# Scans of a four-direction state-space layer: the place of one exponential in ScalarE's queue

## The chip, the cores and the metric

The kernel runs on one core of one Trainium2 chip. The metric is the device time of one execution in microseconds (us). A change under about 0.2% can't be told from no change in this kernel.

## The reference

Two layers work on x, (4, 64, 64, 128) in float32: an attention, a recurrent layer, a selective scan in four directions, and a layer of experts. The change lies in the selective scan, whose core is, for each image b, direction k and channel d (256 channels, 16 states each, 4096 positions):

```
dt = softplus(dts + dt_proj_b)
def step(h, (dt_l, u_l, B_l, C_l)):
    dA = exp(dt_l[..., None] * A)
    h  = h * dA + (dt_l * u_l)[..., None] * B_l
    y  = einsum('bkdn,bkn->bkd', h, C_l)
```

The kernel computes the softplus of a value s as the larger of two numbers: ln(1 + e^s), and a lower bound 1 / (e^-s + 0.5).

## The kernel before, in words

The work of the scans stage (function `scans`) is cut into 132 **windows**: four directions, 33 windows each, of 4 blocks of 125 positions from the four images laid end to end. Of each window 16 **tiles** are scanned: four groups of states (4 of the 16 each), and in a group one tile for each of the four blocks. A tile holds 128 channels on the partitions, times 2 halves of the channels, 4 states and 127 columns, 1016 elements in a row.

One loop over p (the **turn**) writes out the order of all engines by hand, under `manual_schedule`: each engine executes its instructions in the order in which the loop issues them. Group g has the tiles at turns 4g + (g mod 2) + 0, 2, 4, 6, so two groups are interleaved and a tile's successor in its own group comes two turns later. Turns are counted within 16 here, since all repeats from window to window. At turn p the loop issues in this order:

- `finish` (at one turn of a window): a copy of the finished sums on ScalarE (L1415).
- `fill` of tile p+1: TensorE multiplies out the inputs of the scan into one of two PSUM buffers db (L1319), which the scan of tile p-1 must have left.
- `carry` of tile p-1: a small copy on ScalarE (L1364) of the last column of that tile's states into the decays of the tile that continues it. For the first three tiles of a group this is the tile two turns on (p+1 at the time of issue), for the last tile it is the first tile of the same states in the next window, ten turns after the tile. Tile 11 is the last of its group (5, 7, 9, 11); tile 12 is the third of its group (8, 10, 12, 14) and is continued by tile 14.
- `scan` of tile p on VectorE (L1343), which needs its db, its decays and the column carried in.
- sums on TensorE (L1394), the products with C on GpSimd (L1377), and a load of a later row of C on SyncE's queue.
- `decay`: up to three exponentials of decays on ScalarE (L1284), for a group that is scanned later.
- the steps of `project`, a generator which prepares a later window. Each `yield -n` in it says at which turn, counted from the window's own first one, the next step is issued; a step takes its place behind all else of its turn.

The steps of `project` around the change, all on ScalarE, work on tiles of 128 x 1000 elements. `pts` is a PSUM view that holds s; `e` and `bound` are SBUF tiles (`bound` is a view of the tile that the profile calls low; `pts` is a view of mm):

- turn -22 (10 within the window being scanned): `bound` = e^-s (L1200) and e = e^s (L1203), each with a maximum-check sum (`accum_out`).
- turn -21 (11): `bound` = ln(bound + 0.5) (L1205), `pts` = ln(1 + e) (L1206).
- turn -20 (12): `bound` = exp(-bound) (L1208), the last step of the lower bound.
- turns -19 and -18 (13 and 14): dt = max(`pts`, `bound`), in two halves on VectorE (L1214), each behind that turn's scan.
- turn -17: dt times u on GpSimd (L1217), turn -14 and -13: the diagonals of B on VectorE (L1232) and ScalarE (L1248).

`decay` issues three exponentials at turn 12, ahead of the step of turn -20, three at turn 13 and two at turn 14, all for the group whose first tile is scanned at turn 16. `flag` isn't None in the version that runs here; the other branch is for inputs out of range.

Of the kernel before, what the change touches and what calls it, by code (L numbers as in the profile page):

```python
# [20 lines left out]
AF = mybir.ActivationFunctionType  # L21
# [977 lines left out]
def scans(ctx, tc, a, us, ys, flag):  # L999
# [10 lines left out]
    nc = tc.nc  # L1010
# [126 lines left out]
    def in_halves(of):  # L1137
        return of.rearrange("p h (j t) -> p h j t", j=2)

    def project(v):  # L1140
# [46 lines left out]
        bound = in_halves(low[:, : ND * W].rearrange("p (h t) -> p h t", h=ND))  # L1187
        e = in_halves(e)
        if flag is None:
            nc.scalar.activation(e, pts, AF.Relu, scale=-1.0, bias=most)  # L1190
            nc.scalar.activation(e, e, AF.Exp, scale=-1.0, bias=most)
            nc.scalar.activation(bound, e, AF.Copy, scale=-0.5, bias=1.0)
            yield -21
            nc.gpsimd.tensor_mul(bound, bound, e)
            for h in range(ND):
                nc.vector.tensor_max(bound[:, h], pts[:, h], bound[:, h])
            nc.scalar.activation(pts, e, AF.Ln, bias=1.0)
        else:
            nth = todo.index(v)
            nc.scalar.activation(  # L1200
                bound, pts, AF.Exp, scale=-1.0, accum_out=largest[:, 1, nth : nth + 1]
            )
            nc.scalar.activation(e, pts, AF.Exp, accum_out=largest[:, 0, nth : nth + 1])  # L1203
            yield -21
            nc.scalar.activation(bound, bound, AF.Ln, bias=half)  # L1205
            nc.scalar.activation(pts, e, AF.Ln, bias=1.0)  # L1206
            yield -20
            nc.scalar.activation(bound, bound, AF.Exp, scale=-1.0)  # L1208
        yield -19
        v.dt = work.tile([P, ND, W], F32, tag="dt", name="dt")  # L1210
        dt = in_halves(v.dt)
# [16 lines left out]
        for turn, i in ((-14, 0), (-13, 2)):  # L1228
# [18 lines left out]
            for t in range(FEW + 4 * h, FEW + 4 * h + 4):  # L1247
# [4 lines left out]
                    scale=ident32[:, t : t + 1],  # L1252
# [181 lines left out]
    with tc.manual_schedule():  # L1434
# [3 lines left out]
        def projections(p):  # L1438
            nth, turn = divmod(p + BEFORE, TILES)
            if turn == 0 and nth < len(todo):  # L1440
                v = todo[nth]
                v.steps, v.starts = project(v), nth * TILES
                v.goes_on = next(v.steps)
                running.append(v)
            for v in list(running):
                while v.goes_on is not None and p - v.starts >= v.goes_on:
                    v.goes_on = next(v.steps, None)
                if v.goes_on is None:
                    running.remove(v)
# [455 lines left out]
```

## Time and profile before

| what | us |
|---|---|
| runs: median of 3 (lowest, highest) | 9323.02 (9310.93, 9323.11) |
| the profiled execution's own time | 9321.16 |
| its span, from the first to the last instruction | 9319.2 |
| first scan to last scan of the stage (2112 scans) | from 3598.6 to 8650.2 of the span |
| VectorE busy from 3595 to 8655 | 4960.65 of 5060 |
| GpSimd, TensorE, ScalarE busy there | 4842.52, 4798.82, 4536.72 |

The profile is of one execution. PE is TensorE, DVE is VectorE, ACT is ScalarE, POOL is GpSimd. A row of a timeline gives start, length, engine, line, operation, output and input, and the number of instructions that were merged into it. In brackets stands how long the engine stood idle before it, and whose work it waited for. An instruction's length runs on for about 0.07 to 0.1 us after its engine has taken the next one, so lengths add up to a little more than the time they take. In a merged row the length reaches from the first start to the last end.

### The profile page before, as it was taken

The numbers are of one execution on the slowest core, as the hardware profiler recorded it, in microseconds if no ns is written. First come the engines' busy times: TensorE is split into PE (matmuls) and PEld (weight loads), VectorE is DVE, ScalarE is ACT, GpSimd is POOL, SyncE is SP. The second block draws the span as 40 slices with busy tenths as digits, with TensorE's granted clock in tenths as the row PEclk, the third lists the DMA queues.
The fourth block names the chain that finished last, engine by engine and source line by source line (L and its number), as shares of the span: only waits on it lengthen the run. The fifth ranks groups of instructions, "written<-read, shape, count | busy, mean of one in ns | idle before, by whom it ended". The sixth has DMA issues, their size and how long they took to land. (4 is left out here: it accounts for less than half of the span.)

```text
span 9319.2 us, 241459 instructions
## 1 busy us (share of the span) xinstructions
PE 8594.7 (92%) x103250; PEld 4327.6 (46%) x103250; DVE 8279.5 (89%) x5102; ACT 7300.2 (78%) x12114; POOL 4960.2 (53%) x2433
## 2 busy tenths in 40 slices
PE   7999999999989886999999999999999999999766
PEld 3333333333323334555555555555555555555223
DVE  6999999999978415999999999999999999999754
ACT  3888888888856457999999998889999999898321
POOL 0000000000001015999999999999999999999100
PEclk8999999999989887999999999999999999999877
DMA  4000001000011234666666655566666666666624
GB/s 168 39 8 35 8 8 37 8 8 8 8 53 50 107 124 141 178 177 179 180 180 165 165 163 162 164 172 177 179 180 180 179 179 176 175 178 171 238 105 186
DMA packets 533040, 1164.78 MB, mean 125 GB/s; under 512 B 78930, under 2 KB 446546, under 8 KB 504164
## 3 DMA queue, kind: packets, MB, share of 16 engines
q1 hardware_dynamic: 531940, 1149.09, 41.7%
q8 instruction: 815, 13.35, 0.6%
q14 instruction: 285, 2.33, 0.1%
HBM read 828.29 MB, written 182.15 MB: 108 GB/s over the span
## 5 line engine op out<-in xcount | busy, mean ns | idle before, releaser
L1343 DVE TENSOR_TENSOR_SCAN states<-decays,db 128x1016 f32<-128x1016 f32 x2112 | 4657.3, 2255 | 45.8 <-PE db L1319 17.6
L1377 POOL TENSOR_TENSOR products<-states,c_ring 128x1000 f32<-128x1000 f32 x2112 | 4454.1, 2160 | 215.7 <-DVE states L1343 183.8
L1284 ACT ACTIVATE decays<-dt,a_logs 128x500 f32<-128x500 f32 x4224 | 3021.2, 715 | 87.3 <-DVE states L1343 1.2
L1319 PEld LDWEIGHTS db<-b_diag,dtu_t 32*128 32x128 f32 x16896 | 2048.0, 187 | 1388.7 <-DVE states L1343 1208.8
L1319 PE MATMUL db<-b_diag,dtu_t 32*128 32x128 f32 x16896 | 2438.3, 283 | 259.5 <-DVE states L1343 239.9
L1319 PE MATMUL db<-b_other,dtu_t 32*128 32x128 f32 x16896 | 2438.0, 283 | 0.0
L1328 PE MATMUL y<-zeros 32*128 32x128 f32 x14720 | 2123.2, 283 | 0.0
L1319 PEld LDWEIGHTS db<-b_other,dtu_t 32*128 32x128 f32 x16896 | 2047.6, 187 | 1.6
L1394 PE MATMUL y<-products,ident 64*64 64x500 f32 x16896 | 2022.3, 592 | 0.3 <-POOL products L1377 0.3
L1328 PEld LDWEIGHTS y<-zeros 32*128 32x128 f32 x14720 | 1773.4, 186 | 0.0
L342 DVE TENSOR_TENSOR total<-total,ring 128x2048 f32<-128x2048 f32 x768 | 1706.6, 2283 | 32.4 <-ACT ring L304 31.7
masks.py:197 POOL MEMSET ident<- 128x128 f32 x6 | 1.2, 205 | 2915.7 <-SPq L181 2623.3
L304 ACT ACTIVATE ring<-sa 128x2048 f32<-128x2048 f32 (+3 forms) x667 | 1153.7, 1738 | 274.6 <-PE sa L289 263.0
L314 PE MATMUL av<-ring,v_at 128*32 128x256 f32 (+1 forms) x16128 | 1096.3, 389 | 6.2 <-ACT o L323 5.7
L1394 PEld LDWEIGHTS y<-products,ident 64*64 64x64 f32 x16896 | 541.8, 132 | 697.4 <-issue 569.8
L314 PEld LDWEIGHTS av<-ring,v_at 128*32 128x32 f32 x16128 | 421.5, 109 | 951.6 <-issue 749.6
L304 ACT ACTIVATE ring<-sb 128x1536 f32<-128x1536 f32 (+2 forms) x585 | 800.7, 1375 | 73.0 <-PE sb L289 62.8
L289 PE MATMUL sa<-q_at,k_at 32*128 32x512 f32 x4898 | 701.7, 641 | 20.9 <-issue 14.8
L289 PE MATMUL sb<-q_at,k_at 32*128 32x512 f32 x3294 | 623.3, 640 | 0.0
L1248 ACT ACTIVATE b_diag<-mm,ident 128x64 f32<-128x64 f32 x1056 | 261.5, 375 | 322.9 <-DVE b_diag L1232 308.2
L1364 ACT COPY decays<-states 128x8 f32<-128x8 f32 x2048 | 405.2, 198 | 99.9 <-DVE states L1343 98.3
L289 PEld LDWEIGHTS sa<-q_at,k_at 32*128 32x128 f32 x4898 | 192.3, 183 | 354.8 <-issue 177.4
(218 smaller groups left out, 8069.9 us busy)
## 6 DMA issues: line engine op xcount, KB each, us to landing
c_ring<-c_rows SPq DMA_DIRECT2D x2112, 250.0 KB, 5.0
b_other<-b_diag SPq DMA_DIRECT2D x264, 512.0 KB, 5.2
weights<-in_w SPq DMA_DIRECT2D x32, 1024.0 KB, 13.0
u<-u_r SPq DMA_DIRECT2D x60, 500.0 KB, 6.5
y_r<-sum SPq DMA_DIRECT2D x60, 500.0 KB, 5.6
u<-u_c SPq DMA_DIRECT2D x60, 500.0 KB, 6.4
y_c<-sum SPq DMA_DIRECT2D x60, 500.0 KB, 5.3
x<-x SPq DMA_DIRECT2D x96, 256.0 KB, 2.6
```

Source lines behind the costliest of these rows:

```text
L289: nc.tensor.matmul(s[:, m, :], k[rows, tokens(t)], q[rows, chunk(chunk_state["c"])], start=True, stop=True,)
L304: nc.scalar.activation(ring[:, lo : lo + n, :], s[:, at : at + n, :], AF.Exp)
L314: nc.tensor.matmul(chunk_state["av"][rows, some], chunk_state["v"][:, t, rows], ring[:, at + i, some], start=t == 0, stop=t == NJ - 1 and ...
L342: nc.vector.tensor_add(sums[g % 2], sums[g % 2], w)
L1248: nc.scalar.activation(v.b_diag[:, :, :, t].rearrange("p s n -> p (s n)"), b_ps.rearrange("p s n -> p (s n)"), AF.Identity, scale=ident32[ ...
L1284: nc.scalar.activation(to, dt, AF.Exp, scale=scale)
L1319: nc.tensor.matmul(bank.rearrange("p (n t) -> p n t", n=4)[:, :, to : to + 32], v.dtu[rows, h, s, :], b[rows, s, 4 * self.q : 4 * self.q + ...
L1328: nc.tensor.matmul(y[:, idle // 2, :P], zeros[rows], zeros[rows], start=False, stop=False)
L1343: nc.vector.tensor_tensor_scan(order(self.slot(states)), order(self.slot(decays, shift)), order(self.db[:, SKIP + shift :][:, : 2 * LANE]) ...
L1364: nc.scalar.copy(self.edge(later.slot(decays), later.v.into), last)
L1377: nc.gpsimd.tensor_mul(to, h, c)
L1394: nc.tensor.matmul(to, ident[rows, rows], of, start=begins, stop=ends)
```

## The change

The step `bound` = exp(-bound) is issued at turn -21 instead of -20, between the two logarithms. The turn -20 has no step any more. No instruction is added or taken away, and nothing else moves.

```
@@ -1203,9 +1203,8 @@
             nc.scalar.activation(e, pts, AF.Exp, accum_out=largest[:, 0, nth : nth + 1])
             yield -21
             nc.scalar.activation(bound, bound, AF.Ln, bias=half)
+            nc.scalar.activation(bound, bound, AF.Exp, scale=-1.0)
             nc.scalar.activation(pts, e, AF.Ln, bias=1.0)
-            yield -20
-            nc.scalar.activation(bound, bound, AF.Exp, scale=-1.0)
         yield -19
```

ScalarE's order from turn 11 to turn 13 was: carry of tile 10, ln for the bound, ln(1+e), carry of tile 11, three decays, exp for the bound, carry of tile 12. It becomes: carry of tile 10, ln for the bound, exp for the bound, ln(1+e), carry of tile 11, three decays, carry of tile 12.

More of the change, by code (lines that the diff above doesn't have):

```diff
@@ L1205, in project @@
             nc.scalar.activation(bound, bound, AF.Ln, bias=half)
+            nc.scalar.activation(bound, bound, AF.Exp, scale=-1.0)
             nc.scalar.activation(pts, e, AF.Ln, bias=1.0)
-            yield -20
-            nc.scalar.activation(bound, bound, AF.Exp, scale=-1.0)
         yield -19
```

## The prediction

> **What bounds the kernel now.** I read the page first, for the stage that holds the change. Its slices give one digit per engine (tenths busy in 40 equal slices):
>
> ```profile
> PE   7999999999989886999999999999999999999766
> DVE  6999999999978415999999999999999999999754
> ACT  3888888888856457999999998889999999898321
> POOL 0000000000001015999999999999999999999100
> ```
>
> From slice 16 on, where the scans run, all four engines show 8 or 9, so none is free and the question is which one holds up the others in each turn. VectorE's waits from 3595 to 8655 us (the stage) answer it for the engine with the most work:
>
> ```profile
> DVE dt L1214 <- ACT low L1208: 62.7, 124, 14.0
> DVE states L1343 <- PE db L1319: 17.6, 12, 3.0
> DVE states L1343 <- ACT decays L1284: 3.1, 3, 2.3
> ```
>
> Columns: total us, times, longest. VectorE's one regular wait is that of the maximum (L1214) for the exponential which the change moves (L1208): 124 times, of which two come before the first scan (windows 0 and 1, the 14.0 among them), so 122 in the steady run. Then I read a window of 38.2 us, VectorE first:
>
> ```profile
> 6018.62 0.53 DVE L1232 TENSOR_TENSOR b_diag<-mm,ident 128x384 f32<-128x384 f32 x1
> 6019.15 22.15 DVE L1343 TENSOR_TENSOR_SCAN states<-decays,db 128x1016 f32<-128x1016 f32 x10
> 6041.66 0.68 DVE L1214 TENSOR_TENSOR dt<-mm,low 128x500 f32<-128x500 f32 x1 [0.35 <-ACT low L1208]
> 6042.25 2.26 DVE L1343 TENSOR_TENSOR_SCAN states<-decays,db 128x1016 f32<-128x1016 f32 x1
> 6044.43 0.65 DVE L1214 TENSOR_TENSOR dt<-mm,low 128x500 f32<-128x500 f32 x1
> ```
>
> The ten scans are tiles 4 to 13, the one at 6042.25 is tile 14. And ScalarE over the same turns:
>
> ```profile
> 6036.34 0.20 ACT L1364 COPY decays<-states 128x8 f32<-128x8 f32 x1
> 6036.43 1.13 ACT L1205 ACTIVATE low<-low,half 128x1000 f32<-128x1000 f32 x1
> 6037.46 1.00 ACT L1206 ACTIVATE mm<-e 128x1000 f32<-128x1000 f32 x1
> 6038.39 0.20 ACT L1364 COPY decays<-states 128x8 f32<-128x8 f32 x1
> 6038.48 2.22 ACT L1284 ACTIVATE decays<-dt,a_logs 128x500 f32<-128x500 f32 x3
> 6040.60 1.02 ACT L1208 ACTIVATE low<-low 128x1000 f32<-128x1000 f32 x1
> 6041.53 0.19 ACT L1364 COPY decays<-states 128x8 f32<-128x8 f32 x1
> ...
> 6047.29 0.20 ACT L1364 COPY decays<-states 128x8 f32<-128x8 f32 x1 [0.51 <-DVE states L1343]
> ```
>
> ScalarE runs without a pause from the second diagonal of B (L1232 ends at 6019.15) to 6047.29: over these turns it, and not VectorE, sets the pace. The exponential ends at 6040.60 + 1.02 = 6041.62, and the maximum starts 0.04 later.
>
> **The change, step by step.** *What the wait costs now.* The last of the ten scans ends at 6019.15 + 22.15 = 6041.30 and, being 2.25 long (the scan group's mean is 2255 ns), started at 6039.05. VectorE takes an unheld instruction 2.18 after a scan's start (6042.25 to 6044.43). So the maximum could start at 6041.23 and starts at 6041.66: 0.43 lost, a little more than the 0.35 of idle shown, since the scan's tail overlaps.
>
> *What becomes of it.* The maximum will need only the two logarithms and the exponential, all ahead of the carry of tile 11. The three together take 6036.43 to 6038.39 plus one exponential (6040.60 to 6041.53 is 0.93): done by about 6039.5, some 1.7 us before VectorE asks. This wait goes wholly.
>
> *What is late next.* The scan of tile 14 follows the maximum by 0.59 (6041.66 to 6042.25) and could start at 6041.82. But it needs the carry of tile 12, the copy that starts at 6041.53, and ends at 6041.72. Scans that are released by such a copy start 0.08 to 0.09 after its end: the copy before the scan at 6019.15 starts at 6018.86, takes 0.21 and so ends at 6019.07. With the same instructions in front of it, this copy would release the scan at 6041.81, just in time.
>
> *What the order itself costs.* The moved exponential reads and overwrites what the logarithm in front of it has just written. Before, ln(1+e) and four more instructions stood between. An instruction that isn't held starts about 0.10 before the former ends (L1205 ends at 6037.56, L1206 starts at 6037.46). One that waits for its predecessor doesn't: the three decays take 2.22, against 3 x 0.715 = 2.145, so 0.04 of gap at each of two steps. The difference, 0.10 + 0.04 = 0.14, is what I take for the new dependence; from below it is 0 (no wait is needed), from above some 0.2 (a dependence over a longer write, half as much again). No other pair changes its kind. So the carry of tile 12 ends at 6041.86 and releases the scan of tile 14 at 6041.94 to 6041.95. Against 6042.25 that is 0.31 gained a window, with 0.43 at the 0 end (VectorE itself then decides) and 0.24 at the 0.2 end.
>
> A rule bears on this step: the Trainium skill, "ScalarE: Activation LUTs", section "What ACT_TABLE_LOAD costs", says that back-to-back activations overlap by about 93 ns. The rows of unheld pairs agree (0.10), those of the decays, which are back to back too, don't (a gap of 0.04). By the rule alone the sum would be the 0 end.
>
> *Who else is delayed.* ln(1+e), the carry of tile 11 and the three decays come 0.93 + 0.14 = 1.07 later. ln(1+e) then ends at about 6039.5, as said. The carry of tile 11 feeds tile 21, since 11 is the last of its group, ten turns off. The three decays end at about 6041.8 and are for tile 16, scanned after 6047. None of them is on the path; if the carry of tile 11 were, see the slower rival. From the carry of tile 12 on, ScalarE is 0.14 later than now: its next carry (6043.73, for the scan at 6045.00) has over 0.7 to spare now and still has 0.5, since that scan moves to 6044.69. No DMA is moved, nor anything on SyncE's, GpSimd's or TensorE's queue.
>
> *Does the gain last?* ScalarE stands idle 0.51 at 6047.29 for a scan's end; 0.31 + 0.14 = 0.45 fits into that, so it then shifts with VectorE. Later in the window it waits 2.3 us for the diagonals, which VectorE sets. GpSimd waits for scans after its long row:
>
> ```profile
> 6044.59 2.15 POOL L1377 TENSOR_TENSOR products<-states,c_ring 128x1000 f32<-128x1000 f32 x1 [0.81 <-DVE states L1343]
> 6047.34 2.16 POOL L1377 TENSOR_TENSOR products<-states,c_ring 128x1000 f32<-128x1000 f32 x1 [0.59 <-DVE states L1343]
> ```
>
> That is 1.40 a window, of which 0.31 is used up. TensorE stands still for scans' ends after tiles 13, 14, 15 and 3 (L1319 waits for the states), so its chain starts anew from VectorE behind the change and shifts too. So the whole window becomes 0.31 shorter, about 37.8 instead of 38.15.
>
> *Sum.* 122 x 0.31 = 38 us. Against the profiled execution's 9321.2 this gives 9283; the runs' median is 1.9 higher, so 9285 in its terms. The ends: 122 x 0.43 = 52 (9271) and 122 x 0.24 = 29 (9294).
>
> **The rivals.** *The exponential isn't held by the logarithm* (the rule above): 9271, with a chance of 0.12. Only the decays' spacing speaks against it, and that is of other tiles.
>
> *The gain is absorbed*: the window is set elsewhere, by the PSUM fills (12 waits of scans for them, 17.6 us), or the order on ScalarE comes out as before. Then 9323. Against it: the waits of ScalarE, GpSimd and TensorE for VectorE, each longer than 0.31 a window in total. Chance 0.08.
>
> *The carry of tile 11 is wanted at once* (slower). If the scan of tile 13 needed it, as most scans need the copy one turn before, it would end at 6038.59 + 1.07 = 6039.66 and release the scan at 6039.74 instead of 6039.05, 0.69 late. With the maximum's wait gone (0.43) the window is 0.26 longer: 122 x 0.26 = 32 us, 9355. It decides as soon as the scan of tile 13, or anything before the maximum, is held by more than 0.43. For it: ScalarE has no pause in these turns, so all behind the moved step is 1 us late. Against it: the numbering of the tiles, and that the trace shows that scan unheld today. Chance 0.06, other things that make it slower included.
>
> **How the numbers follow.** The forecast has 0.74: 9285. About 0.2% (18.6 us) is what a measurement here can tell from no change, so faster means below 9304.4. Forecast and first rival lie there: 0.86. Same: 0.08. Slower: 0.06. The range reaches from below the first rival, as the runs differ among themselves by 12 us, to the edge of "same": 9264 to 9304. The absorbed and the slower case stay outside, with 0.14.
>
> **What the profile after should show.** The wait of L1214 for L1208 is gone from VectorE's list. The exponential starts about 0.04 after the end of the logarithm before it, ln(1+e) follows. The scan of tile 14 starts about 0.6 to 0.7 after the maximum, and 0.08 after the end of a carry; windows are 37.8 apart. Wrong: a new wait of the scan of tile 13 or 12 for ScalarE (the slower rival), a longer wait of L1319 or of scans for db (absorbed), the exponential 0.1 before the logarithm's end with windows of 37.7 (first rival).

## The result, and the profile after

The kernel with the change takes 9279.8 us (median of 5 runs, 9276.8 to 9283.0) against 9316.2 us before (median of 5, 9310.9 to 9323.1). The ratio is 0.9960, with a 95% interval from 0.9949 to 0.9971: faster, by 27 to 48 us, or 0.3 to 0.5%. The profiled execution took 9277.8 us, its span is 9275.8 against 9319.2, and the stage of the scans, from the first scan to the last, went from 5051.6 to 5010.3 us: 41 of the 43 us lie there.

In the new file the lines behind the change have moved up by one: the scan is L1342, the maximum L1213, the carry L1363, the decays L1283, the moved exponential is L1206 and ln(1+e) L1207. These are VectorE's longest waits in the stage (total us, times, longest):

```profile
DVE states L1342 <- issue: 11.2, 61, 0.4
DVE states L1342 <- PE db L1318: 10.2, 8, 2.2
DVE states L1342 <- ACT decays L1283: 7.7, 5, 4.6
```

The line on top of the list before, the maximum for the exponential, is gone. The new first line is not harmless: "issue" is where the list could name nobody, and the timeline shows who it is. VectorE in the same turns of one window:

```profile
5957.85 0.53 DVE L1231 TENSOR_TENSOR b_diag<-mm,ident 128x384 f32<-128x384 f32 x1
5958.39 22.15 DVE L1342 TENSOR_TENSOR_SCAN states<-decays,db 128x1016 f32<-128x1016 f32 x10
5980.45 0.65 DVE L1213 TENSOR_TENSOR dt<-mm,low 128x500 f32<-128x500 f32 x1
5981.19 2.27 DVE L1342 TENSOR_TENSOR_SCAN states<-decays,db 128x1016 f32<-128x1016 f32 x1
5983.37 0.65 DVE L1213 TENSOR_TENSOR dt<-mm,low 128x500 f32<-128x500 f32 x1
```

And ScalarE:

```profile
5975.66 1.14 ACT L1205 ACTIVATE low<-low,half 128x1000 f32<-128x1000 f32 x1
5976.83 1.04 ACT L1206 ACTIVATE low<-low 128x1000 f32<-128x1000 f32 x1
5977.77 0.99 ACT L1207 ACTIVATE mm<-e 128x1000 f32<-128x1000 f32 x1
5978.70 0.19 ACT L1363 COPY decays<-states 128x8 f32<-128x8 f32 x1
5978.79 2.21 ACT L1283 ACTIVATE decays<-dt,a_logs 128x500 f32<-128x500 f32 x3
5980.91 0.19 ACT L1363 COPY decays<-states 128x8 f32<-128x8 f32 x1
```

The first maximum starts while the tenth scan's tail still runs (5958.39 + 22.15 = 5980.54), so it waits for nothing. The exponential starts 0.03 after the end of its logarithm (5975.66 + 1.14 = 5976.80). The carry of tile 12 ends at 5981.10 and the scan of tile 14 starts 0.09 later, 0.74 after the maximum, where VectorE alone needs 0.57 (5983.37 to the next scan at 5983.94). So the wait for the exponential has become a shorter wait for the carry. It hardly shows in the list, because it runs for the most part under the maximum's own length. The visible rest is 0.06 to 0.10 us of idle time in the windows of the first two directions, which are the first half of the stage, and about 0.17 in those of the last two; the 61 waits of the list are nearly all of the second kind, and the first kind isn't in it.

### The profile page after: what moved, and what is told of

Same layout as the page of the kernel before. It is cut to its first block, busy times and chain, and to the rows that moved or that the text cites. A ratio compares the mean times of both kernels' runs of the same rounds, so it can differ in the third digit from the quotient of the medians.

```text
span 9275.8 us, 241458 instructions
## 1 busy us (share of the span) xinstructions
PE 8579.3 (92%) x103250; PEld 4320.6 (47%) x103250; DVE 8275.9 (89%) x5102; ACT 7319.4 (79%) x12114; POOL 4960.7 (53%) x2433
## 5 line engine op out<-in xcount | busy, mean ns | idle before, releaser
L1342 DVE TENSOR_TENSOR_SCAN states<-decays,db 128x1016 f32<-128x1016 f32 x2112 | 4658.7, 2256 | 58.4 <-issue 11.2
L1283 ACT ACTIVATE decays<-dt,a_logs 128x500 f32<-128x500 f32 x4224 | 3020.6, 715 | 87.4 <-DVE states L1342 1.2
L1363 ACT COPY decays<-states 128x8 f32<-128x8 f32 x2048 | 404.3, 197 | 38.7 <-DVE states L1342 32.4
```

Source lines behind the costliest of these rows:

```text
L1283: nc.scalar.activation(to, dt, AF.Exp, scale=scale)
L1342: nc.vector.tensor_tensor_scan(order(self.slot(states)), order(self.slot(decays, shift)), order(self.db[:, SKIP + shift :][:, : 2 * LANE]) ...
L1363: nc.scalar.copy(self.edge(later.slot(decays), later.v.into), last)
```

## The experiments

The theory: after the change the path runs along ScalarE's queue, from the second diagonal of B to the carry of tile 12; all that stands in front of this carry costs its full length, and 0.13 us of that is the exponential's wait for the logarithm that it now follows. The rivals were that the order on ScalarE costs nothing, and that something other than ScalarE holds the window after the change. Below, "windows apart" is the median distance between the scans of tile 4 of neighbouring windows in the trace; it is 38.14 us before and 37.85 with the change. All distances are from start to start, and medians over the windows of the trace.

**1. The exponential behind ln(1+e).**

```
             nc.scalar.activation(bound, bound, AF.Ln, bias=half)
-            nc.scalar.activation(bound, bound, AF.Exp, scale=-1.0)
             nc.scalar.activation(pts, e, AF.Ln, bias=1.0)
+            nc.scalar.activation(bound, bound, AF.Exp, scale=-1.0)
```

> The exponential of the bound stays at turn -21, but behind ln(1+e) instead of in front of it, so that it no longer follows the logarithm that it reads. Theory (the carry of tile 12 releases the scan of tile 14, and the exponential held by the logarithm before it costs ScalarE 0.13 us): the carry ends 0.13 us sooner, the scan of tile 14 starts 0.58 to 0.60 us after the maximum instead of 0.74, windows are 37.70 to 37.73 us apart instead of 37.85, and the time is 122 to 129 times 0.13 to 0.15 us shorter than with the change: 9260 to 9265 us against 9280. Rival (the order among the three costs nothing; what is left after the change is set by VectorE or by the fills of db): 9280 as with the change, windows 37.85 apart.

Measured: 9259.7 us, ratio to before 0.9943 (0.9929 to 0.9957), windows 37.71 apart. The interval overlaps that of the change a little, but the rows on ScalarE differ as expected:

```profile
5957.83 1.13 ACT L1205 ACTIVATE low<-low,half 128x1000 f32<-128x1000 f32 x1
5958.86 1.00 ACT L1206 ACTIVATE mm<-e 128x1000 f32<-128x1000 f32 x1
5959.79 1.03 ACT L1207 ACTIVATE low<-low 128x1000 f32<-128x1000 f32 x1
5960.71 0.20 ACT L1363 COPY decays<-states 128x8 f32<-128x8 f32 x1
5960.81 2.22 ACT L1283 ACTIVATE decays<-dt,a_logs 128x500 f32<-128x500 f32 x3
5962.93 0.19 ACT L1363 COPY decays<-states 128x8 f32<-128x8 f32 x1
```

From the start of the first logarithm to that of the carry of tile 12 are 5.10 us, against 5.25 with the change. The second instruction now starts 0.10 before the first one ends. That is the dependence of the changed order, measured: 0.13 to 0.15 us a window, for the same six instructions. The step from a logarithm to an exponential isn't what costs: here it stands between L1206 and L1207, which don't depend on each other, and the exponential starts 0.07 before the logarithm's end. VectorE's scan of tile 14 still starts 0.09 after the end of the carry, so ScalarE's queue sets the window in this version too.

**2. The kernel before, with two decays a turn later.** The exponential stays at turn -20.

```
-            12: [(4, (0, 1, 2))],
-            13: [(4, (3, 4, 5))],
-            14: [(4, (6, 7))],
+            12: [(4, (0, 1))],
+            13: [(4, (2, 3, 4))],
+            14: [(4, (5, 6, 7))],
```

> The kernel before, with the exponential of the bound where it was (turn -20), but one decay exponential of turn 12 moved to turn 13 and one of turn 13 to turn 14. Theory (all that matters is how much work ScalarE has in front of the exponential and of the carry of tile 12, not where the exponential itself stands): the exponential ends 0.75 us sooner, the maximum finds it done, the carry of tile 12 comes 0.75 us after the exponential as before and in time, and VectorE decides: 0.42 to 0.46 us a window, 9258 to 9265 us. Rival (the gain needs the exponential at the earlier turn): 9316 as before.

Measured: 9252.8 us, ratio 0.9931 (0.9918 to 0.9945), windows 37.68 apart. The total is 5 us below the expected range; the account of the prediction below says why. The interval lies below that of the change. ScalarE's exponential, and VectorE's maximum and scan of tile 14:

```profile
5967.82 1.02 ACT L1208 ACTIVATE low<-low 128x1000 f32<-128x1000 f32 x1
```

```profile
5969.18 0.65 DVE L1214 TENSOR_TENSOR dt<-mm,low 128x500 f32<-128x500 f32 x1
5969.75 2.26 DVE L1343 TENSOR_TENSOR_SCAN states<-decays,db 128x1016 f32<-128x1016 f32 x1
```

The exponential ends at 5968.84, 0.34 before the maximum, and the scan follows the maximum by 0.57. Taking one decay from in front of the exponential gains more than moving the exponential.

**3. The change, with the same shift of decays.**

> The kernel with the change, and the same shift of two decays by one turn. Theory: the carry of tile 12 comes 0.75 us sooner, although the exponential still waits for its logarithm; the scan of tile 14 follows the maximum by 0.58 to 0.60 us, windows 37.70 us apart, 9258 to 9265 us, as without the dependence. Rival (the dependence itself or VectorE's own pace holds the window at 37.85): 9280.

Measured: 9250.2 us, ratio 0.9928 (0.9915 to 0.9942), windows 37.68 apart; again the total is below the expected range, by 8 us. VectorE, around the maximum:

```profile
5945.51 22.15 DVE L1342 TENSOR_TENSOR_SCAN states<-decays,db 128x1016 f32<-128x1016 f32 x10
5967.57 0.65 DVE L1213 TENSOR_TENSOR dt<-mm,low 128x500 f32<-128x500 f32 x1
5968.14 2.26 DVE L1342 TENSOR_TENSOR_SCAN states<-decays,db 128x1016 f32<-128x1016 f32 x1
```

The scan follows the maximum by 0.57, as after the second maximum of each window: nothing holds it. The dependence is still there (the exponential starts 0.03 after its logarithm), but no longer costs anything.

**4. The change, with one copy more in front of the carry of tile 12.**

```
             nc.scalar.activation(pts, e, AF.Ln, bias=1.0)
+            yield -20
+            nc.scalar.copy(spare, zeros)
```

The line that sets up the tile `spare` isn't shown.

> The kernel with the change, and one copy of 128x128 elements more on ScalarE at the end of turn 12 (from zeros into a spare tile that nobody reads), behind the three decays and in front of the carry of tile 12. It takes some 0.20 to 0.28 us of ScalarE's time. Theory: the carry and the scan of tile 14 move by the whole of it, 129 times 0.20 to 0.28 = 26 to 36 us: 9306 to 9316 us. Rival (ScalarE isn't what holds the window after the change): 9280.

Measured: 9302.3 us, ratio 0.9985 (0.9976 to 0.9994), windows 38.06 apart, 0.20 more than with the change. ScalarE and VectorE, the extra copy at L1210:

```profile
6001.35 0.28 ACT L1210 COPY spare<-zeros 128x128 f32<-128x128 f32 x1
6001.53 0.20 ACT L1366 COPY decays<-states 128x8 f32<-128x8 f32 x1
```

```profile
6000.89 0.66 DVE L1216 TENSOR_TENSOR dt<-mm,low 128x500 f32<-128x500 f32 x1
6001.82 2.27 DVE L1345 TENSOR_TENSOR_SCAN states<-decays,db 128x1016 f32<-128x1016 f32 x1 [0.28 <-issue]
```

The copy takes 0.18 of ScalarE's time, the carry ends at 6001.73 and the scan starts 0.09 after it. The whole of it goes into the window, so ScalarE is the path after the change. The total is 22 us above that of the change, where 129 x 0.20 would be 26, and 4 us below the expected range; the ten runs of this version spread over 22 us, so the windows say more than the total. Again the waiting is put down to "issue".

**5. Experiments 1 and 3 together.**

> Both edits together: the exponential of the bound at turn -21 behind ln(1+e), and the two decays one turn later. Theory (with either edit the scan of tile 14 already waits for nothing but VectorE): no more than the shift of the decays alone, the scan of tile 14 at 2.73 us after that of tile 13, windows 37.68 us apart, 9248 to 9254 us. Rival (each edit removes a cost of its own on ScalarE, so that they add up): another 0.13 us a window, 37.55, some 9235 us.

Measured: 9250.6 us, ratio 0.9931 (0.9917 to 0.9944), windows 37.68 apart. The two edits don't add up: both work on the same wait, and the distance from tile 13 to tile 14 is 2.73 as in experiment 3.

**6. Experiment 3, with the copies of b_rows a turn later.** This went beyond the change, to see what is late next.

```
-        yield -30
+        yield -29
         b_rows = ...
```

> The kernel with the change and the two decays one turn later, and the copies of b_rows (two, 0.84 us together) at turn -29 instead of -30, so that the carry of tile 2 comes in front of them. This carry holds the scan of tile 4 today: it ends 0.09 us before that scan starts, and VectorE itself would be ready about 0.08 us sooner. Theory: the wait before tile 4 goes, but TensorE fills without a pause from the end of the scan of tile 3 to the fill of tile 14, and the scans of tiles 8 and 12 wait for it now (2.39 and 2.30 us after the scan before, against 2.16 to 2.19 elsewhere), so the 0.08 us come back there: windows 37.68 us apart as without this edit, 9246 to 9254 us. Rival (ScalarE is still what holds the window): 0.08 us a window, 37.60, some 9240 us.

Measured: 9359.9 us, ratio 1.0047 (1.0034 to 1.0061), windows 38.50 apart. Both expectations were wrong, in size and sign. The wait before tile 4 did go (2.63 us after the scan of tile 3, against 2.71), but VectorE's waits now begin with

```profile
DVE states L1342 <- ACT decays L1363: 103.6, 194, 1.0
```

and ScalarE shows why:

```profile
5993.28 0.65 ACT L1254 COPY quarters<-dtu 128x512 f32<-128x512 f32 x1
5993.80 0.23 ACT L1363 COPY decays<-states 128x8 f32<-128x8 f32 x1
5995.10 0.99 ACT L1247 ACTIVATE b_diag<-mm,ident 128x64 f32<-128x64 f32 x4 [1.07 <-DVE b_diag L1231]
5995.91 0.74 ACT L1254 COPY quarters<-dtu 128x256 f32<-128x256 f32 x2
5996.67 0.83 ACT L1171 COPY b_rows<-xd 16x256 f32<-16x256 f32 x2
...
5999.73 0.19 ACT L1363 COPY decays<-states 128x8 f32<-128x8 f32 x1
```

The two copies had been executed in time that ScalarE would otherwise have spent waiting for the second diagonal. Moved behind it, they leave 1.07 us idle in front of it and lie at the head of the stretch without pause, whose carries come 0.84 later: the scan of tile 6 starts 0.68 us later after that of tile 5 than it did, and that of tile 10 starts 0.48 later after that of tile 9. What the expectation said of TensorE, that it would give the gain back at tiles 8 and 12, was not put to the test by this.

## Why the prediction was right

*What the wait cost.* The distance from the scan of tile 13 to that of tile 14 is 2.73 us when nothing holds it (experiments 2, 3 and 5). Before, it was 3.19 in the windows of the first two directions and 3.29 in those of the last two. So the wait cost 0.46 and 0.56. The prediction worked out 0.43 from one window, which lies in the first half; the row showed 0.35 of idle, since most of the rest lies under the scan's tail. The two halves differ at tile 12, whose scan starts 2.31 after that of tile 11 in the first and 2.21 in the second; why is open. As long as ScalarE sets the window, the 0.10 only lengthens VectorE's wait at tile 14, and the windows of both halves are equally long: 38.14 before, 37.86 and 37.85 with the change, 37.71 and 37.70 in experiment 1. In experiments 2 and 3, where this wait is gone, they are 37.68 or 37.69 and 37.59. This is why these two came out below their expected ranges, which took 0.46 at most for every window, and why the gain of the change doesn't depend on the half.

*The dependence.* Estimated at 0.14, with 0 to 0.2 as ends. The exponential starts 0.03 after the logarithm's end, against 0.10 before it for pairs without a wait: 0.13. The two activations back to back, of which the second waits for the first, don't overlap, as the spacing of the decays had shown (each of them starts 0.03 after the end of the one that it waits for). The Trainium skill's figure ("ScalarE: Activation LUTs", section "What ACT_TABLE_LOAD costs": back-to-back activations overlap by about 93 ns) holds for the pair without a dependence in experiment 1, 0.10, and not for this one.

*What is late next.* The carry of tile 12 was named, with its release of the scan 0.08 to 0.09 later; measured 0.09. The gain of a window was put at 0.31; the distance from tile 13 to tile 14 fell by 0.30 (3.19 to 2.89 in the first half, 3.29 to 2.99 in the second), and the window by 0.29 (38.14 to 37.85), since the second maximum has the next scan start 0.01 later. 122 x 0.29 = 35 us is what the regular windows give, and the runs' medians show 36, between two kernels whose runs spread over 12 and 6 us. The 41 of the stage are 36 from 126 such windows and nearly 6 from five others, which differ between the two traces by 1.2 to 2.6 us each, four of them shorter and one longer; that the change does this isn't shown.

*The rivals.* An exponential that isn't held would have made windows of 37.7; they are 37.85. Experiment 1, in which the hold is gone, took 9259.7, where this rival put 9271: the rival's base alone is 5 too high (9317.7 in the runs beside this experiment), and the five runs spread over 23 us. That the carry of tile 11 is wanted at once is refuted by the trace: this copy starts at 5978.70, and the scan of tile 13, the last of the ten, starts about 5978.29 (5980.54 less its 2.25), before it. The gain isn't absorbed either: GpSimd's wait for tile 14 shrank, as the working had it:

```profile
5983.54 2.14 POOL L1376 TENSOR_TENSOR products<-states,c_ring 128x1000 f32<-128x1000 f32 x1 [0.49 <-DVE states L1342]
5986.28 2.16 POOL L1376 TENSOR_TENSOR products<-states,c_ring 128x1000 f32<-128x1000 f32 x1 [0.60 <-DVE states L1342]
```

The total, 9285 against 9279.8, is off by 5 us, and its base alone is 7 too high: the median of the runs before that it started from was 9323.0, and with two runs more it is 9316.2, from which the same 38 us lead to 9278.

*What the prediction didn't see* is that another edit of the same size does more. It weighed the place of the exponential; what mattered was the total of ScalarE's work in front of the carry of tile 12, and one decay taken from there (0.75 us) ends the wait whatever the exponential's place. The fastest versions, experiments 2, 3 and 5, take 9250 to 9253 us, 0.7% below the kernel before; they can't be told apart.

What is left in the window without this wait is VectorE's own work and three short waits. In experiment 3 the scans of tiles 8 and 12 start 2.39 and 2.30 us after their predecessors, against 2.16 to 2.19 at the other scans from tile 5 to 13. Both start 0.145 after the end of the last matmul of their fill in nearly all windows, where the other scans of this stretch start 0.34 to 1.43 after theirs, and TensorE doesn't pause ahead of these two fills. So they wait for TensorE. The scan of tile 4 starts 0.09 after its carry, and in experiment 6, where this carry comes sooner, 0.09 earlier. What taking away the waits at tiles 8 and 12 would gain wasn't tried.

## What to carry to other kernels

Where an engine with a hand-written order runs without pause from one meeting point with another engine to the next, look for the instruction that the other engine waits for last and take work from ahead of it; here that gained more (experiment 2) than a better place for one instruction (the change). Don't put an instruction directly behind the one whose result it reads when another can stand between, and don't move work out of a stretch in which the engine waits anyway (experiment 6 lost 1.2% against experiment 3 by it). When a wait leaves the list, look at start-to-start distances too: a wait that runs under the tail of the instruction before it shows little idle time and can be missing from the list. Look at them by stretches as well: one median over the whole stage hid that the last two directions had more to gain than the first two.

## What the runs showed of the hardware

On ScalarE a dependent activation of 128x1000 starts 0.03 us after its predecessor's end, an independent one 0.07 to 0.10 before it. A scan on VectorE that waits for a copy of 128x8 on ScalarE starts 0.09 us after the copy's end, in the kernel before (tile 4), with the change and with the copy added (tile 14). A copy of 128x128 that takes 0.28 us by its row holds the queue for 0.18. A scan that waits for its fill on TensorE starts 0.145 us after the end of the last matmul of the fill (tiles 8 and 12, experiment 3).
